# Gated mixing of two experts rewritten as (x + a) + g (e − a), with the experts' rows summed by TensorE

## The chip, the core and the metric

The kernel runs on one core of a Trainium2 chip. The metric is the device time of one execution in microseconds (us); the time before is the median of three runs, 3077.14 (3073.25 to 3079.84). A core has five engines with a queue of instructions each: TensorE (PE), VectorE (DVE), ScalarE (ACT), GpSimd (POOL) and SyncE (SP, which issues most transfers). They run side by side and wait for each other through semaphores. Within its own queue an engine takes instructions in order, so one that waits holds all that are queued behind it.

## The reference, cut to what matters

x has 2 batches of 2048 rows of 256. The first layer is attention plus a mixture of experts; the second is a selective state-space layer plus a ternary linear layer.

```python
xn = layernorm(x)
# first layer
x = x + attention(xn) + ffn(xn)
# ffn(x):
xn = layernorm(x) * ln_g + ln_b
abel = gelu(xn @ abel_w + abel_b)                      # "a" in the title
tw, ti = top_k(xn @ gate_w_moe + gate_b_moe, 2); tw = softmax(tw)
moe = sum over the two chosen experts of tw * expert(xn)
nonabel = moe @ rot                                    # "e" in the title
g = sigmoid(concat(abel, nonabel) @ mix_w + mix_b)
return x + abel * (1 - g) + nonabel * g
# second layer
xn = layernorm(x)
x = x + state_space(xn) + ternary_linear(xn)
```

The state-space layer projects xn to 1024 columns, convolves half of them over 4 rows, applies silu, derives a step size dt and vectors B and C, and runs h = exp(dt A) h + dt B x along the rows, for 16 states of each of 512 channels; y sums h C over the states.

## The kernel before, in words

The 4096 rows are 32 tiles of 128, handled as 8 chunks of 512 (QT = 4 tiles). There are four stages.

**First stage** (0 to 183 us). For each chunk it computes the normalised rows n1 and, normalised again, n2, transposes both, and makes q, k, v (q and k are stored to qk_d). The abel rows come from PE through a gelu on ACT (L308) into the tile ab. POOL multiplies ab by its part of mix_w (L311, tile am), DVE reduces that to one number a row (L314, sab), SP stores ab to ab_d (L315). POOL then adds n1 and the bias of the attention's projection to the x rows kept in SBUF (L316, L317). A scheduler makes the order on the engines here; the pools of the stage are given back at its end, and the first tiles of attention (L595 mask, L617 onesr) lie in that room.

**Attention and routing** (to about 1300 us) and the **experts** (to about 1920 us). The experts' results lie in y_d, one row for each token and chosen expert. The x rows with attention added are in xa_d.

**Mixing and state space** (L1148, 1920 to 3079 us). From L1784 on the order on every engine is the program's order. The work is 8 units of 512 rows (4 chunks by 2 batches), each of 16 steps, one per state. A step is: on ACT four decays exp(dt A) for the next step (L1729), on DVE a small add of the carried state (L1841), the scan over 128 x 2048 (L1843) and the product dt·x·B for the next step (L1753), on POOL a copy of the carry (L1854) and the product of the states with C (L1855), on PE the spreading of B's row for the product (L1740, tile bb) and the y sums (L1770).

Between these, three generators per unit are woven in by hand. `mix` makes the rows that enter the second layer, `ahead` the projections, convolution (L1446 on PE, L1455 on ACT, silu L1461), dt (L1535), B and C of the next unit, and `behind` the gate (L1590 on POOL) and the output of the unit before. The lists `kinds` and `kinds0` (L1657, L1672; the second for the first unit) name, for each generator, the step and quarter of a step at which it goes on to its next `yield`. A unit's mixing runs two units ahead of its scans, a gather of its rows (L1302, eight indirect transfers on POOL's queue) three ahead. The places of one unit's mixing:

| place (step, quarter) | what is issued in mix |
|---|---|
| (8,0) to (11,2), (14,1), (15,1), a unit earlier | gathers L1302, scaling by the router's weights on ACT L1311 |
| (0,2) | mo = sum of the two experts' rows on POOL, L1316; loads of ab and of the x rows xc |
| (3,2) and (4,0) | transposes of mo, L1327, first and second half |
| (4,2) | gate matmuls L1335, L1338, sigmoid on ACT L1348, L1349 |
| (7,1), (8,0) | reciprocal L1355, 1 − g on ACT L1356; pn = mo·rot L1362 in two halves, xc += g·pn on DVE L1369 |
| (8,0), (8,2) | ab scaled by 1 − g on ACT L1376; xc += ab on POOL L1379 |
| (9,1) to (12,3) | layer normalisation and transposes (L1384 to L1410) |

PSUM results of these flows take turns in two buffers (`mm`). What reads a result (a copy on ACT, say) is not issued with the matmuls but held by `issued` until the next result is issued, or until `settle`. So a result's reader stands in its engine's queue where the next one begins. The transposed rows moT take the place of the second expert's rows:

```python
moT = ys[:, 1].rearrange("p (k i) d -> p k (i d)", k=2)
```

The first two units' mixing runs ahead of the scans, the first one serially (1940 to 1957 us).

Of the kernel before, what the change touches and what calls it, by code (L numbers as in the profile page):

```python
# [13 lines left out]
AF = mybir.ActivationFunctionType  # L14
ALU = mybir.AluOpType
# [4 lines left out]
P = 128  # L20
# [13 lines left out]
TOP = 2  # L34
# [67 lines left out]
def tile_model(ctx: ExitStack, tc: tile.TileContext, t, out):  # L102
    nc = tc.nc
# [15 lines left out]
    ident = const.tile([P, P], F32, name="ident")  # L119
# [3 lines left out]
    rot = const.tile([P, 2, D], F32, name="rot")  # L123
# [27 lines left out]
    QT = CH // P  # L151
# [6 lines left out]
    with ExitStack() as c0:  # L158
# [5 lines left out]
        ab_d = scr.tile([P, NT, D], F32, name="ab_d")  # L164
# [3 lines left out]
        with tc.tile_pool(name="vs", bufs=1) as vsp, tc.tile_pool(name="qk", bufs=3) as qk:  # L168
# [6 lines left out]
            with tc.tile_pool(name="pa", bufs=2) as pa, tc.tile_pool(  # L175
# [4 lines left out]
                for c in range(NCH):  # L180
                    xg = xa[:, c * QT : (c + 1) * QT, :]
# [37 lines left out]
                for c in range(NCH):  # L219
                    xg = xa[:, c * QT : (c + 1) * QT, :]  # L220
# [13 lines left out]
                    for k in range(2):  # L234
                        p1 = pa_ps.tile([P, CH], F32, tag="tr", name=f"p1_{c}_{k}")
                        p2 = pa_ps.tile([P, CH], F32, tag="tr", name=f"p2_{c}_{k}")
                        for i in range(QT):
# [8 lines left out]
                            scale=col("ln_g")[:, k : k + 1],  # L246
                            bias=col("ln_b")[:, k : k + 1],
# [4 lines left out]
                    for i, name in enumerate(("q", "k")):  # L252
                        for m in range(2):
                            ps = pa_pa.tile([P, CH], F32, tag="ab", name=f"{name}_{c}_{m}")
                            for k in range(2):
                                nc.tensor.matmul(
                                    ps,
                                    lhsT=wd[i][:, k, m * P : (m + 1) * P],
                                    rhs=x1[:, k, :],
                                    start=(k == 0),  # L260
                                    stop=(k == 1),
                                )
                            parts = pa.tile([P, 2, CH], F32R, tag="parts", bufs=3, name=f"{name}p_{c}_{m}")
                            bias = bd[i][:, m : m + 1]
# [11 lines left out]
                    for h in range(2):  # L276
                        ps = pa_pa.tile([P, 2, D], F32, tag="ab", name=f"v_{c}_{h}")
                        for j in range(2):
                            at = (2 * h + j) * P
                            for k in range(2):  # L280
                                nc.tensor.matmul(
                                    ps[:, j, :],
                                    lhsT=x1[:, k, at : at + P],
                                    rhs=wv[:, k, :],
                                    start=(k == 0),
                                    stop=(k == 1),
# [9 lines left out]
                    ab = pa.tile([P, QT, D], F32, tag="ab", name=f"ab_{c}")  # L296
                    for i in range(QT):
                        ps = pa_pa.tile([P, D + E], F32, tag="ab", name=f"abp_{c}_{i}")
                        for k in range(2):
                            nc.tensor.matmul(  # L300
                                ps,
                                lhsT=x2[:, k, i * P : (i + 1) * P],
                                rhs=aw[:, k, :],
                                start=(k == 0),
                                stop=False,
# [4 lines left out]
                    am = pa.tile([P, QT, D], F32, tag="am", name=f"am_{c}")  # L310
# [1 line left out]
                        am, ab, row("mix_w")[:, 0:D].unsqueeze(1).to_broadcast([P, QT, D]), ALU.mult  # L312
                    )
                    nc.vector.tensor_reduce(sab[:, c * QT : (c + 1) * QT], am, AX.X, ALU.add)  # L314
                    nc.sync.dma_start(ab_d[:, c * QT : (c + 1) * QT, :], ab)  # L315
                    nc.gpsimd.tensor_tensor(xg, xg, n1, ALU.add)  # L316
                    nc.gpsimd.tensor_tensor(  # L317
                        xg, xg, row("b_proj").unsqueeze(1).to_broadcast([P, QT, D]), ALU.add
                    )
# [828 lines left out]
def mix_and_state_space(tc, t, col, row, ident, ones, rot, routes, sab, rw, y_d, ab_d, xa_d, out_tiles):  # L1148
# [10 lines left out]
    nc = tc.nc  # L1159
    NC = S // CH  # L1160
    QT = CH // P
# [5 lines left out]
    with ExitStack() as ctx:  # L1167
# [80 lines left out]
        ps = ps_m.tile([P, 1], F32, tag="mm", name="absum")  # L1248
# [20 lines left out]
        def settle(n=0):  # L1269
            while len(held) > n:  # L1270
                take, ps = held.pop(0)
                take(ps)
# [21 lines left out]
        def mix(at):  # L1294
# [14 lines left out]
            for e in range(TOP):  # L1309
# [2 lines left out]
                        ys[:, e, i, :], ys[:, e, i, :], AF.Copy, scale=wts[:, e, n0 + i : n0 + i + 1]  # L1312
                    )
                yield
            mo = ys[:, 0]
            nc.gpsimd.tensor_tensor(mo, mo, ys[:, 1], ALU.add)  # L1316
            ab = one.tile([P, QT, D], F32, tag="k", name=f"ab_{u}")
            nc.sync.dma_start(ab, ab_d[:, n0 : n0 + QT, :])
            xc = m_["xc"] = xcp.tile([P, QT, D], F32, tag="xc", name=f"xc_{u}")
# [4 lines left out]
            for k in range(2):  # L1324
                ps = mm(f"moT_{u}_{k}")
                for i in range(QT):
                    nc.tensor.transpose(  # L1327
                        ps[:, i * P : (i + 1) * P], mo[:, i, k * P : (k + 1) * P], ident
                    )
                issued(ps, lambda ps, k=k: nc.scalar.copy(moT[:, k, :], ps))  # L1330
                yield
            settle()

            ps = mm(f"gate_{u}", (P, QT))
            nc.tensor.matmul(ps, lhsT=ident, rhs=sab[:, n0 : n0 + QT], start=True, stop=False)  # L1335
            for i in range(QT):
                for k in range(2):
# [4 lines left out]
                        start=False,  # L1342
# [10 lines left out]
            settle()  # L1353
            yield
            nc.vector.reciprocal(g[:, 0, :], g[:, 1, :])  # L1355
            nc.scalar.activation(g[:, 1, :], g[:, 0, :], AF.Identity, scale=-1.0, bias=1.0)  # L1356
            for h in range(2):
                ps = mm(f"pn_{u}_{h}", (P, 2, D))
                for i in range(2):
                    ts = slice((2 * h + i) * P, (2 * h + i + 1) * P)  # L1360
                    for k in range(2):
                        nc.tensor.matmul(  # L1362
                            ps[:, i, :], lhsT=moT[:, k, ts], rhs=rot[:, k, :], start=(k == 0), stop=(k == 1)
                        )

                def add(ps, h=h):
                    for i in range(2):
                        n = 2 * h + i
                        nc.vector.scalar_tensor_tensor(  # L1369
                            xc[:, n, :], ps[:, i, :], g[:, 0, n : n + 1], xc[:, n, :], ALU.mult, ALU.add  # L1370
                        )

                issued(ps, add)
                yield
            for i in range(QT):
                nc.scalar.activation(ab[:, i, :], ab[:, i, :], AF.Copy, scale=g[:, 1, i : i + 1])  # L1376
            yield
            settle()
            nc.gpsimd.tensor_tensor(xc, xc, ab, ALU.add)  # L1379
            yield  # L1380

            mv = one.tile([P, QT, 2], F32, tag="mv", bufs=2, name=f"mv3_{u}")
# [584 lines left out]
```

## Time and profile before

| what | us | share of the span |
|---|---|---|
| median of the runs | 3077.14 | |
| the profiled execution | 3080.93 | |
| its span | 3079.2 | |
| PE busy | 2634.9 | 86% |
| DVE busy | 2043.7 | 66% |
| ACT busy | 1592.4 | 52% |
| POOL busy | 1187.6 | 39% |

By stages, busy time of the engines and the granted clock of PE (1 is full speed):

| stretch, us | PE | DVE | ACT | POOL | clock |
|---|---|---|---|---|---|
| 0 to 183 | 144.0 | 106.5 | 73.3 | 60.0 | 0.95 |
| 183 to 1300 | 1015.8 | 860.2 | 653.9 | 175.6 | 0.95 |
| 1300 to 1920 | 601.7 | 104.7 | 162.0 | 98.9 | 0.99 |
| 1920 to 2014 | 50.5 | 29.6 | 39.1 | 24.0 | 0.69 |
| 2014 to 3057 | 806.0 | 942.7 | 662.3 | 824.2 | 0.80 |

A row of groups reads: line, engine, operation, tile written <- tiles read, shapes, count | busy us, mean ns | idle time before it and what ended most of it. A row of waits reads: engine, tile and line that waited <- engine, tile and line waited for: us in total, times, longest. A row of a timeline reads: start us, duration us, engine, line, operation, count and, in brackets, idle time before it and what ended that. A row of stretches has, for each of PE, PE's weight loads, DVE, ACT and POOL, the busy us and the number of instructions, then the granted clock, DMA's share and GB/s.

### The profile page before, as it was taken

To read this page: it belongs to the slowest core of one execution; us is meant where nothing else is said; L and a number is where in the kernel's file an instruction comes from. 1 tells how busy PE (TensorE), PEld (TensorE's weight loads), DVE (VectorE), ACT (ScalarE), POOL (GpSimd) and SP (SyncE) were. 2 spreads that over 40 slices of the span, in tenths; PEclk is the share of its full clock that TensorE was granted. 3 is DMA by queue.
4 is the path that set the end of the run, shared out by engine and by line. 5 is a ranking of instruction groups with operands and counts; after the bars stand their busy time and mean duration, and the time that the engine had idled before them with its cause. 6 is when DMAs were issued, how large, how long until landed. Compare 5 with 4: busy or idle time off the path is not lost. (4 is left out here: it accounts for less than half of the span.)

```text
span 3079.2 us, 39986 instructions
## 1 busy us (share of the span) xinstructions
PE 2634.9 (86%) x15021; PEld 1493.3 (48%) x15021; DVE 2043.7 (66%) x2558; ACT 1592.4 (52%) x2546; POOL 1187.6 (39%) x934
## 2 busy tenths in 40 slices
PE   6887888999999999799999999577778888788747
PEld 4543433445444444488888888333333343333303
DVE  6576766888788888324111011258999999999996
ACT  3424555666566666422222222456766676666643
POOL 4313223010111011111111111247887978878775
PEclk9978988999999999899999999677887888879758
DMA  8843214112232220434345553323544535445350
GB/s 290 214 133 80 57 51 86 29 29 42 50 48 29 29 29 1 151 134 144 133 150 194 183 193 109 77 54 85 120 111 104 131 78 133 110 102 117 82 116 14
DMA packets 120614, 309.58 MB, mean 101 GB/s; under 512 B 28464, under 2 KB 70832, under 8 KB 102880
## 3 DMA queue, kind: packets, MB, share of 16 engines
q1 hardware_dynamic: 100496, 206.57, 28.3%
q0 software_dynamic: 18576, 99.24, 9.6%
q8 instruction: 122, 2.00, 0.3%
q10 hardware_dynamic: 1344, 1.16, 0.1%
q14 instruction: 76, 0.62, 0.1%
HBM read 228.51 MB, written 78.38 MB: 100 GB/s over the span
## 5 line engine op out<-in xcount | busy, mean ns | idle before, releaser
L758 ACT ACTIVATE p<-s 128x1024 f32<-128x1024 f32 (+3 forms) x640 | 563.2, 900 | 382.4 <-PE s L750 361.5
L665 DVE TENSOR_REDUCE best<-m 128x2 f32<-128x1024 f32 (+3 forms) x640 | 669.6, 1062 | 111.6 <-PE m L652 101.0
L1855 POOL TENSOR_TENSOR hh<-hh,cc 128x2048 f32<-128x2048 f32 x128 | 579.9, 4531 | 10.3
L1843 DVE TENSOR_TENSOR_SCAN hh<-decay,uh 128x2048 f32<-128x2048 f32 x128 | 565.9, 4421 | 23.8 <-ACT decay L1729 10.1
L705 PE MATMUL pv<-p,v 128*17 128x256 f32 (+1 forms) x4608 | 383.8, 379 | 49.0 <-POOL p L763 46.1
L763 POOL TENSOR_SCALAR_AFFINE_SELECT p<-p 128x256 f32<-128x256 f32 x256 | 103.3, 408 | 785.6 <-ACT p L758 784.5
L1729 ACT ACTIVATE decay<-dd,a_neg 128x511 f32<-128x511 f32 x512 | 332.9, 712 | 53.4 <-DVE hh L1843 52.8
L1118 ACT ACTIVATE hT<-h,b1s 128x256 f32<-128x256 f32 x296 | 137.7, 473 | 384.3 <-PE h L1111 384.3
L1132 DVE TENSOR_TENSOR yt<-o,b 128x512 f32<-128x512 f32 x37 | 25.6, 692 | 436.9 <-PE o L1124 436.9
L1753 DVE TENSOR_TENSOR uh<-dd,bb 128x2048 f32<-128x2048 f32 x128 | 293.6, 2294 | 21.5 <-PE bb L1740 11.6
L750 PE MATMUL s<-q,k 64*128 64x512 f32 (+3 forms) x1280 | 288.2, 437 | 22.9 <-DVE best L665 17.6
L652 PE MATMUL m<-k,q 64*128 64x512 f32 (+3 forms) x1280 | 281.6, 426 | 17.6 <-DVE best L665 8.9
L1111 PE MATMUL h<-xT,w 128*128 128x256 f32 x1184 | 276.1, 387 | 19.7 <-ACT hT L1118 8.1
L1124 PE MATMUL o<-w,hT 128*128 128x256 f32 x1184 | 262.7, 380 | 0.0
L1074 POOL DMA_INDIRECT w<-in_w,wrow x74 | 71.1, 961 | 479.2 <-PE h L1111 255.5
L1111 PEld LDWEIGHTS h<-xT,w 128*128 128x128 f32 x1184 | 226.7, 193 | 54.8 <-ACT hT L1118 8.5
L750 PE MATMUL s<-tops,onesr 64*128 64x512 f32 (+3 forms) x1280 | 248.5, 371 | 0.0
L1124 PEld LDWEIGHTS o<-w,hT 128*128 128x128 f32 x1184 | 225.7, 191 | 30.9
L1770 PE MATMUL y<-hh,sel 128*32 128x512 f32 x1024 | 162.1, 710 | 78.8 <-POOL hh L1855 78.6
L705 PEld LDWEIGHTS pv<-p,v 128*17 128x17 f32 x4608 | 107.9, 97 | 232.4 <-issue 113.5
L750 PEld LDWEIGHTS s<-q,k 64*128 64x128 f32 x1280 | 127.0, 188 | 168.1 <-DVE best L665 56.6
L652 PEld LDWEIGHTS m<-k,q 64*128 64x128 f32 x1280 | 129.3, 192 | 131.7 <-ACT p L758 68.1
(341 smaller groups left out, 3477.2 us busy)
## 6 DMA issues: line engine op xcount, KB each, us to landing
dd<-dd_d SPq DMA_DIRECT2D x120, 512.0 KB, 7.1
q<-qk_d SPq DMA_DIRECT2D x128, 128.0 KB, 5.1
k<-qk_d SPq DMA_DIRECT2D x128, 128.0 KB, 7.5
x_d<-zero SPq DMA_DIRECT2D x6, 1664.0 KB
xg<-x_d SPq DMA_DIRECT2D x37, 256.0 KB, 6.6
y_d<-yt SPq DMA_DIRECT2D x37, 256.0 KB
qk_d<-qp SPq DMA_DIRECT2D x16, 512.0 KB, 7.3
qk_d<-kp SPq DMA_DIRECT2D x16, 512.0 KB, 4.0
```

The costliest lines, as they stand in the source:

```text
L652: nc.tensor.matmul(ps[:, h, 0:n], lhsT=qT[hs, qs], rhs=kT[hs, c * CH : c * CH + n], start=True, stop=True, tile_position=(HP * h, 0),)
L665: nc.vector.tensor_reduce(best[:, i, :, c], ps[:, :, 0:n], AX.X, ALU.max)
L705: nc.tensor.matmul(pv[r0 : r0 + HS + 1, lo - f * HC : HC], lhsT=v[:, b * TPB + kb, 2 * pr + h, :], rhs=pt[:, h, lo:hi], start=(kb == 0), s ...
L750: nc.tensor.matmul(ps[:, h, off:CH], lhsT=(kT[hs, kb * P : (kb + 1) * P], onesr[hs, :])[i], rhs=(qT[hs, j * CH + off : (j + 1) * CH], tp[h ...
L758: nc.scalar.activation(pt[:, :, off:CH], ps[:, :, off:CH], AF.Exp, scale=float(HS) ** -0.5)
L1111: nc.tensor.matmul(ph, lhsT=w1[:, k * DF + f * P : k * DF + (f + 1) * P], rhs=xT[:, k, :], start=(k == 0), stop=(k == 1),)
L1124: nc.tensor.matmul(po[:, h, :], lhsT=hT[:, f, h * P : (h + 1) * P], rhs=w2[:, f * D : (f + 1) * D], start=(f == 0), stop=(f == NF - 1),)
L1729: nc.scalar.activation(decay[G % 2][:, q, 1:], of[at]["dd", n // 4][:, 0, q, 1:], AF.Exp, scale=a_neg[:, q, n : n + 1],)
L1753: nc.vector.tensor_tensor(uh, of[at]["dd", n // 4][:, 1], of[at]["bb", n].to_broadcast(full), ALU.mult)
L1770: nc.tensor.matmul(of[at]["y"][C4 * q : C4 * (q + 1), :], lhsT=sel, rhs=hh[:, q, :], start=False, stop=(g == 3), tile_position=(0, C4 * q),)
L1843: nc.vector.tensor_tensor_scan(hh.rearrange("p q c -> p (q c)"), decay[G % 2].rearrange("p q c -> p (q c)"), uh.rearrange("p q c -> p (q c)"),
L1855: nc.gpsimd.tensor_tensor(hh, hh, m_["cc", g].to_broadcast(full), ALU.mult)
```

## The change

The mixed row is x + a + g (e − a) in place of x + g e + (1 − g) a. The first stage adds a to the x rows that it keeps (POOL) and stores −a in place of a (negated on ACT, into the tile am). In the mixing, pn becomes the sum of −a, by a matmul with the identity, and of the product with rot, both in PSUM; 1 − g, the four scalings of ab and the addition of ab to xc go. The addition of the two experts on POOL goes too: each transpose of their sum becomes two matmuls with the identity, which add up in PSUM. Both halves are now issued at the place (3,2), and the place (4,0) has nothing of the mixing.

```diff
@@ first stage
                     nc.vector.tensor_reduce(sab[:, c * QT : (c + 1) * QT], am, AX.X, ALU.add)
-                    nc.sync.dma_start(ab_d[:, c * QT : (c + 1) * QT, :], ab)
+                    nc.scalar.activation(am, ab, AF.Copy, scale=-1.0)
+                    nc.sync.dma_start(ab_d[:, c * QT : (c + 1) * QT, :], am)
                     nc.gpsimd.tensor_tensor(xg, xg, n1, ALU.add)
+                    nc.gpsimd.tensor_tensor(xg, xg, ab, ALU.add)
@@ mix
-            mo = ys[:, 0]
-            nc.gpsimd.tensor_tensor(mo, mo, ys[:, 1], ALU.add)
...
             for k in range(2):
                 ps = mm(f"moT_{u}_{k}")
                 for i in range(QT):
-                    nc.tensor.transpose(
-                        ps[:, i * P : (i + 1) * P], mo[:, i, k * P : (k + 1) * P], ident
-                    )
+                    for e in range(TOP):
+                        nc.tensor.matmul(
+                            ps[:, i * P : (i + 1) * P],
+                            lhsT=ys[:, e, i, k * P : (k + 1) * P],
+                            rhs=ident,
+                            start=(e == 0),
+                            stop=(e == TOP - 1),
+                        )
                 issued(ps, lambda ps, k=k: nc.scalar.copy(moT[:, k, :], ps))
-                yield
+            yield
+            yield
             settle()
...
             nc.vector.reciprocal(g[:, 0, :], g[:, 1, :])
-            nc.scalar.activation(g[:, 1, :], g[:, 0, :], AF.Identity, scale=-1.0, bias=1.0)
...
                     ts = slice((2 * h + i) * P, (2 * h + i + 1) * P)
+                    nc.tensor.matmul(
+                        ps[:, i, :], lhsT=ident, rhs=ab[:, 2 * h + i, :], start=True, stop=False
+                    )
                     for k in range(2):
                         nc.tensor.matmul(
-                            ps[:, i, :], lhsT=moT[:, k, ts], rhs=rot[:, k, :], start=(k == 0), stop=(k == 1)
+                            ps[:, i, :], lhsT=moT[:, k, ts], rhs=rot[:, k, :], start=False, stop=(k == 1)
                         )
...
-            for i in range(QT):
-                nc.scalar.activation(ab[:, i, :], ab[:, i, :], AF.Copy, scale=g[:, 1, i : i + 1])
             yield
             settle()
-            nc.gpsimd.tensor_tensor(xc, xc, ab, ALU.add)
             yield
```

## The prediction

> **What bounds the kernel now.** I read the page's busy shares and slices, then its costliest groups, the waits of VectorE (DVE), a table by stretches, and timelines. The state-space stage is the last third, from the first scan at 2014 to 3057 us. The change touches that stage, its prologue (1940 to 2014) and the first stage (0 to 187); attention and experts between them are only displaced. Costliest groups that matter, from the page:
>
> ```profile
> L1855 POOL TENSOR_TENSOR hh<-hh,cc 128x2048 f32<-128x2048 f32 x128 | 579.9, 4531 | 10.3
> L1843 DVE TENSOR_TENSOR_SCAN hh<-decay,uh 128x2048 f32<-128x2048 f32 x128 | 565.9, 4421 | 23.8 <-ACT decay L1729 10.1
> ...
> L1753 DVE TENSOR_TENSOR uh<-dd,bb 128x2048 f32<-128x2048 f32 x128 | 293.6, 2294 | 21.5 <-PE bb L1740 11.6
> ```
>
> 128 steps of 4.42 (scan) + 2.29 (product) + 0.17 (add) + some 0.25 of hand-over make 7.1 us: DVE sets the pace. The stretches view, 2300 to 2500 us, agrees:
>
> ```profile
> 2300.00:2500.00 200.00, 167.06 (x534) 70.25 (x534) 184.54 (x99) 134.80 (x208) 161.92 (x87) 0.82 0.48 115
> ```
>
> DVE is busy 184.5 of 200, POOL 161.9, TensorE (PE) 167.1. Work taken from POOL or ACT therefore pays only where DVE waits for it. Those waits, 2170 to 2950 us:
>
> ```profile
> DVE uh L1753 <- PE bb L1740: 11.1, 11, 1.5
> DVE hh L1843 <- ACT decay L1729: 9.9, 6, 3.0
> DVE xc L1369 <- PE pn L1362: 3.1, 4, 1.4
> ```
>
> About 25 us in all, hardly one named POOL; POOL stands behind PE's part where PE's y sums (L1770) wait for hh (45.8 us in 2100 to 2900) and bb queues behind them. The groups of PE in that stretch show the mixing, and on what it waits:
>
> ```profile
> L1362 PE MATMUL pn<-rot,ys 128*128 128x256 f32 x96 | 35.7, 536 | 0.0
> ...
> L1338 PE MATMUL gate<-rw,ys 128*128 128x1 f32 x96 | 21.3, 343 | 16.4 <-ACT ys L1330 16.4
> ...
> L1327 PE MATMUL moT<-ident,ys 128*128 128x128 f32 x48 | 8.8, 311 | 0.0
> ```
>
> In these 6 units pn's 8 matmuls a unit left 96 records and the 8 transposes 48: an fp32 matmul leaves two records, an fp32 transpose one.
>
> **The transposing sums on PE.** 8 transposes a unit become 16 matmuls, and both halves are issued at place (3,2). At full clock, records of 128 columns start 110 ns apart (4 transposes: 3×0.11+0.33 = 0.66 us in units 1 to 5). Thirty-two take 31×0.11+0.33 = 3.74 us where 0.66 stood before the first copy. In cold records (210 ns) it is 6.9. What this meets, in unit 3, on ACT and then DVE:
>
> ```profile
> 2467.22 0.58 ACT L1330 COPY ys<-moT 128x512 f32<-128x512 f32 x1 [0.89 <-PE moT L1327]
> 2467.83 1.28 ACT L1461 ACT_TABLE_LOAD   x1
> 2469.12 1.91 ACT L1461 ACTIVATE xs<-xs 128x2048 f32<-128x2048 f32 x1
> 2471.04 1.28 ACT L1729 ACT_TABLE_LOAD   x1
> 2472.33 2.56 ACT L1729 ACTIVATE decay<-dd,a_neg 128x511 f32<-128x511 f32 x4
> 2474.80 0.56 ACT L1330 COPY ys<-moT 128x512 f32<-128x512 f32 x1
> ```
> ```profile
> 2475.79 0.17 DVE L1841 TENSOR_TENSOR uh<-uh,c 128x4 f32<-128x4 f32 x1
> 2476.07 4.42 DVE L1843 TENSOR_TENSOR_SCAN hh<-decay,uh 128x2048 f32<-128x2048 f32 x1
> ```
>
> The decays of step 5 end at 2474.89, the scan that needs them starts at 2476.07: 1.18 us of slack. In the changed order ACT's queue has both copies ahead of the silu. The second waits for the burst's end, and the first is held too: it writes half of ys[:,1], which the burst still reads. Queued behind are table, silu, table, four decays. They come 3.74−0.66 = 3.1 us later. Slack is 1.15 to 1.18 in units 1, 3, 4 and none in 2 and 5 (decay end 2347.63, scan 2347.66). Loss: 3×1.95 + 2×3.1 = +12 us at full clock; with records of 210 ns 3×5.1+2×6.2 = +28. I take +12, since all transposes in these units ran at 0.66. POOL's mo add goes ahead of the burst, and with it ACT's copies of cv (14.5 us of waits for POOL's zs) come up to 2.36 earlier; but the last cv stands on PE behind a bb that waits for DVE (2461.47 in unit 3), so the burst doesn't start earlier.
>
> The Trainium skill ("TensorE: Matmul & The Clock Gate", Terms) speaks against this edit: transpose mode is four times faster for FP32. By it one matmul costs four transposes, the burst 64×0.11 = 7.0 us, and the loss 3×5.2+2×6.4 = +28 (an estimate from that page and the 110 ns). The row shows two records per fp32 matmul against one, each of 256 columns starting 220 ns after the last as each transpose of 128 does after 110; the trace decides, a factor of 2. No run here has an fp32 matmul of 128 columns, so +28 stays inside the range.
>
> What comes back: the gate matmuls no longer wait for a second copy that is queued behind the decays. That wait is the 16.4 us of the row above, 2.7 to 4.4 a unit. Starting earlier, the xp, dt, bb, pn chain on PE gains as much, and DVE's gaps at steps 6 and 7 (1.9, 1.6, 0.3, 1.9, 1.6 us in units 1 to 5, 7.2 in all) mostly close: −6.3. The four added matmuls of pn per half (8 records, 0.22 each hot, 0.43 cold) are 1.8 to 3.4 a unit of this lead; PE has some 33 idle us in 200, and I charge nothing unless the lead fails (below).
>
> **What POOL and ACT lose.** Per unit POOL drops two adds of 2.36, ACT a small g and four scalings of 0.49. POOL's products trail the scan by 3.3 to 3.9 us at steps 9 and 10 and by 8.5 at 11; the xc add is one cause. PE's y sum waits for it and the following bb comes 1.2 to 1.4 late at step 13. I take 0.9 back in four units: −3.6 (ends: 0, where the gathers hold POOL, and −6). In unit 0 the one wait of DVE's bn_stats for POOL's xc (1.8 at 2154.7) goes partly: −1.5. Another such wait (5.8 near the first steps) gives nothing: a chain over dt ends at 2050.3 anyway.
>
> **The prologue** is serial: moT at 1942.0 (1.95 us), gate 1943.8 to 1947.8, pn 1947.7 to 1953.2, DVE's xc, POOL's xc 1954.26 for 2.34, bn_stats 1956.6. The burst starts cold, some 5.45 (between 3.74 and 6.9): +3.7 at the gate's end after the pipelined copies; pn gains 8 records, +1.6; POOL's add goes, −2.5. Sum +2.8 (0 to +5). The second chunk's burst lies ahead of other waiting and is hidden.
>
> **The first stage.** Eight times POOL gets one add (2.35), ACT one negation (1.02 by the 128x1024 row of L758), and SP's store of it starts later. In mid-stage the negation waits for DVE's reduce and holds ACT about a microsecond, the store comes some 4.7 later, and the loads of q and k queue behind it on SP; PE or the other stores are later still, so hidden. One row bears on the added POOL adds: a DVE scaling of 128x256 (L144) has a median of 0.406 and a worst of 1.765, ending as a POOL add ended. "Advanced Engine Details and Errata" of the skill (GPSIMD Details) says why: POOL shares a read and a write interface with DVE. Its rule would stall DVE over each of eight adds, up to 8×1.4 = 11; the trace has one or two such outliers in some 24 POOL adds. I take +1.5 (0 to +5).
>
> The end is exposed. POOL's queue, then DVE's:
>
> ```profile
> 179.56 2.34 POOL L311 TENSOR_TENSOR am<-ab,rows 128x1024 f32<-128x1024 f32 x1 [12.01 <-ACT ab L308]
> 183.26 0.29 POOL L595 MEMSET mask<- 128x128 f32 x1 [1.36 <-DMA q<-qk_d]
> ```
> ```profile
> 181.93 1.22 DVE L314 TENSOR_REDUCE sab<-am 128x4 f32<-128x1024 f32 x1 [2.25 <-POOL am L311]
> 183.19 0.23 DVE L617 CAST onesr<-ones 128x128 fp32r<-128x128 f32 x1
> ```
>
> Attention's first tiles lie where the first stage's pools were, and start when the last user is done: the reduce, at 183.15. Now POOL still has +ab to 184.3 and the bias to 186.6, and ACT's negation ends at 184.2 with its store landing by 187.9. The mask waits for ACT and DMA, onesr for POOL and ACT. +3.5 to +4.7, taken +4, and DVE runs without gaps behind it, so it carries to the end.
>
> **Sum.** 1.5 + 4 + 2.8 − 1.5 + 12 − 6.3 − 3.6 = +8.9. The profiled run took 3080.93 (span 3079.2 and 1.7 around it), so 3089.8 on its footing; that run lies 3.8 above the median of 3077.14, from which I forecast 3086.
>
> **Rivals,** each with its chance.
> - *Slow burst* (0.18): fp32 matmuls of 128 columns take 0.21 a record or four passes. The term 12 becomes 28: 3102. For it: cold stretches, granted clock 0.82 in the table. Against: 0.66 in every steady unit.
> - *PE lead fails* (0.12): the longer burst and pn eat the gate's lead, DVE waits for pn and bb at steps 6 to 7 stay. Without the −6.3 and with 0.9 more in each of four units: 3085.9 + 6.3 + 3.6, about 3096.
> - *Faster by a freed POOL* (0.20): it decides on POOL's lag behind the scan at step 11. Falls that from 8.5 below 4, by all that is dropped, then hh is in time for every y sum: the bb and pn waits (11.1 + 3.1) and the small ones (1.5) close, and in unit 0 both POOL waits (5.8 + 1.8). With the burst's 12, the prologue's 2.8, and the hand-over absorbed later by attention: −15.7 − 7.6 + 14.8 = −8.5, 3069. Against: the gathers hold POOL in the same steps, and the waits name PE and ACT.
> - *Nothing measurable* (0.20): the stall at step 5 lets POOL and PE catch up, so that it costs 12 and returns as much from later steps (the 14.2 of bb and pn instead of my 9.9); prologue and first stage at their low ends, 0 and +3.5: 12 − 14.2 + 3.5 − 1.5 = 0, 3077.
> - *Likeliest as summed* (0.30): 3082 to 3092.
>
> The measurement tells 0.2% (6.2 us) from no change, so faster means below 3071, slower above 3083.3. Faster 0.20, same 0.20, slower 0.60 (0.30 + 0.18 + 0.12). The range goes from the freed POOL's to the slow burst's time, 3068 to 3103, and leaves out the far half of each.
>
> **What would show it.** In the changed trace: the moT burst at step 3 near 3.7 us with 32 records (6.9 or 7 is the slow rival); the scan of step 5 waiting for decay 2 to 3 us in each of units 1 to 5; the gate free of ACT's copy and steps 6 and 7 without gaps; onesr near 187; POOL's lag at step 11 under 8. I am wrong if scan 5 starts on time, if POOL's lag falls by its whole 4.7, or if DVE's tensor_scalars in the first stage lengthen under POOL's adds.

## The result, and the profile after

The changed kernel takes 3094.04 us (median of 5 runs, 3091.30 to 3100.57), the kernel before in the same comparison 3076.23 (5 runs, 3073.06 to 3079.84). The ratio is 1.0064, 95% interval 1.0048 to 1.0080: slower by about 18 us. Forecast were 3086, a loss of 9, and a range up to 3103. The direction and the range held; the loss is twice the forecast and lies above the 3082 to 3092 that was given as likeliest.

The profiled execution took 3093.74 (span 3092.0). Code lines lie 5 or 6 lower here than before: the scan L1843 is now L1849, the product L1759, the decays L1735, the copies of moT L1335. The groups of the page:

```profile
L1849 DVE TENSOR_TENSOR_SCAN hh<-decay,uh 128x2048 f32<-128x2048 f32 x128 | 565.9, 4421 | 37.6 <-ACT decay L1735 24.0
L1861 POOL TENSOR_TENSOR hh<-hh,cc 128x2048 f32<-128x2048 f32 x128 | 580.0, 4531 | 11.0 <-PE y L1776 0.4
...
L1759 DVE TENSOR_TENSOR uh<-dd,bb 128x2048 f32<-128x2048 f32 x128 | 293.7, 2295 | 16.4 <-PE bb L1746 7.0
```

Durations are those of before to the nanosecond or two. What moved is idle time: the scan's wait for the decays went from 10.1 to 24.0, the product's wait for PE's bb from 11.6 to 7.0. The waits of DVE between 2170 and 2970 us say the same of the steady units:

```profile
DVE hh L1849 <- ACT decay L1735: 23.8, 10, 3.8
DVE uh L1759 <- PE bb L1746: 4.9, 7, 1.8
DVE xc L1378 <- PE pn L1371: 3.1, 2, 2.3
```

PE's groups of the mixing, 2100 to 2900 us:

```profile
L1371 PE MATMUL pn<-rot,ys 128*128 128x256 f32 x96 | 34.1, 493 | 0.0
L1328 PE MATMUL moT<-ident,ys 128*128 128x128 f32 x192 | 25.5, 296 | 0.0
L1367 PE MATMUL pn<-ab,ident 128*128 128x256 f32 x48 | 21.9, 550 | 0.0
L1345 PE MATMUL gate<-rw,ys 128*128 128x1 f32 x96 | 11.7, 250 | 0.9 <-ACT ys L1335 0.9
```

192 records for 96 matmuls in six units: two for each fp32 matmul. The gate's wait for the copy is gone, 16.4 to 0.9.

A timeline of ACT in unit 3, and DVE's scan behind it:

```profile
2477.09 0.58 ACT L1335 COPY ys<-moT 128x512 f32<-128x512 f32 x1 [3.18 <-PE moT L1328]
2477.98 0.59 ACT L1335 COPY ys<-moT 128x512 f32<-128x512 f32 x1 [0.31 <-PE moT L1328]
2478.58 1.28 ACT L1467 ACT_TABLE_LOAD   x1
2479.88 1.91 ACT L1467 ACTIVATE xs<-xs 128x2048 f32<-128x2048 f32 x1
2481.81 1.28 ACT L1735 ACT_TABLE_LOAD   x1
2483.10 2.56 ACT L1735 ACTIVATE decay<-dd,a_neg 128x511 f32<-128x511 f32 x4
```
```profile
2485.69 4.42 DVE L1849 TENSOR_TENSOR_SCAN hh<-decay,uh 128x2048 f32<-128x2048 f32 x1 [2.15 <-ACT decay L1735]
```

Both copies stand ahead of the silu, the first of them idle for 3.18 us while the burst runs, and the scan of step 5 comes 2.15 late. In unit 2 it is 3.85. The difference is one of PE's clock, as two timelines of PE show:

```profile
2337.74 5.40 PE L1452 MATMUL cv<-xr,taps 128*128 128x512 f32 x8
2343.07 1.06 PE L1776 MATMUL y<-hh,sel 128*32 128x512 f32 x8
2344.07 3.84 PE L1328 MATMUL moT<-ident,ys 128*128 128x128 f32 x32
...
2469.48 3.70 PE L1452 MATMUL cv<-xr,taps 128*128 128x512 f32 x8
2473.11 1.07 PE L1776 MATMUL y<-hh,sel 128*32 128x512 f32 x8
2474.10 3.84 PE L1328 MATMUL moT<-ident,ys 128*128 128x128 f32 x32
```

The burst takes 3.84 in both. The convolution block ahead of it took 5.40 in unit 2, with a granted clock of 0.68, and 3.70 in unit 3, with 1.00.

The stretch from 2300 to 2500 us has DVE busy 180.05 where it was 184.54, and less work on ACT and POOL:

```profile
2300.00:2500.00 200.00, 166.71 (x584) 71.34 (x583) 180.05 (x92) 129.95 (x202) 153.38 (x82) 0.87 0.47 111
```

The end of the first stage, in timelines of POOL and of DVE:

```profile
187.61 2.35 POOL L318 TENSOR_TENSOR xa<-xa,ab 128x1024 f32<-128x1024 f32 x1
190.04 2.34 POOL L319 TENSOR_TENSOR xa<-xa,rows 128x1024 f32<-128x1024 f32 x1
193.53 0.20 POOL L597 MEMSET mask<- 128x128 f32 x1 [1.15 <-DMA ab_d<-am]
```
```profile
187.68 1.22 DVE L314 TENSOR_REDUCE sab<-am 128x4 f32<-128x1024 f32 x1 [2.26 <-POOL am L311]
193.51 0.44 DVE L619 CAST onesr<-ones 128x128 fp32r<-128x128 f32 x1 [4.61 <-DMA ab_d<-am]
```

The reduce is 5.75 later than before, and onesr, which followed it at once, now waits 4.61 more, last for the store of −a.

Where the profiled execution's 12.8 us went, by landmarks in the two traces:

| stretch | before | after | difference |
|---|---|---|---|
| first stage, to the end of its last reduce L314 | 183.15 | 188.90 | +5.75 |
| from there to attention's onesr | 0.04 | 4.61 | +4.57 |
| attention, to the end of its last pv matmul | 1091.3 | 1090.0 | −1.3 |
| to the end of the experts' last matmul | 645.4 | 641.9 | −3.5 |
| to the first scan | 94.3 | 94.5 | +0.1 |
| first scan to end of the last | 1038.3 | 1043.0 | +4.8 |
| behind the last scan | 26.7 | 29.1 | +2.4 |

The experts' row is not the change's. From the first to the last matmul of the experts it was 630.1 before and 624.3 after, and between 626.0 and 630.0 in nine of the runs below that leave that stage alone. This execution was quick there by some 5 us. Nor is the 12.8 the loss: the profiled execution of before lies 4.7 above its median, this one at its own. Rows of single executions carry several us of chance. The stretch from the first scan to the last took 1038.3 and 1032.2 in two executions with the mixing of before (the second is that of the last experiment), and 1038.8 to 1044.7 in the five that have the instructions of the changed mixing: about +6.5 on the mean, where the table has +4.8.

### The profile page after: what moved, and what is told of

The parts are those of the page before. It is cut to its first block, busy times and chain, and to the rows that moved or that the text cites. A ratio compares the mean times of both kernels' runs of the same rounds, so it can differ in the third digit from the quotient of the medians.

```text
span 3092.0 us, 40438 instructions
## 1 busy us (share of the span) xinstructions
PE 2654.0 (86%) x15277; PEld 1517.0 (49%) x15277; DVE 2050.8 (66%) x2558; ACT 1586.3 (51%) x2514; POOL 1170.8 (38%) x926
## 5 line engine op out<-in xcount | busy, mean ns | idle before, releaser
L1849 DVE TENSOR_TENSOR_SCAN hh<-decay,uh 128x2048 f32<-128x2048 f32 x128 | 565.9, 4421 | 37.6 <-ACT decay L1735 24.0
L1735 ACT ACTIVATE decay<-dd,a_neg 128x511 f32<-128x511 f32 x512 | 332.1, 711 | 61.9 <-DVE hh L1849 61.1
L1759 DVE TENSOR_TENSOR uh<-dd,bb 128x2048 f32<-128x2048 f32 x128 | 293.7, 2295 | 16.4 <-PE bb L1746 7.0
```

The source lines that it names most:

```text
L1735: nc.scalar.activation(decay[G % 2][:, q, 1:], of[at]["dd", n // 4][:, 0, q, 1:], AF.Exp, scale=a_neg[:, q, n : n + 1],)
L1759: nc.vector.tensor_tensor(uh, of[at]["dd", n // 4][:, 1], of[at]["bb", n].to_broadcast(full), ALU.mult)
L1849: nc.vector.tensor_tensor_scan(hh.rearrange("p q c -> p (q c)"), decay[G % 2].rearrange("p q c -> p (q c)"), uh.rearrange("p q c -> p (q c)"),
```

## The experiments

Each was timed beside the kernel before; its ratio stands with its interval. "Index n" is the gap of DVE between the end of scan n and the next scan, less what it works in it; its floor is 0.2 to 0.3. Sums of gaps are over units 1 to 5.

**The first stage taken back.**

```diff
-                    nc.scalar.activation(am, ab, AF.Copy, scale=-1.0)
-                    nc.sync.dma_start(ab_d[:, c * QT : (c + 1) * QT, :], am)
+                    nc.sync.dma_start(ab_d[:, c * QT : (c + 1) * QT, :], ab)
-                    nc.gpsimd.tensor_tensor(xg, xg, ab, ALU.add)
```

> The changed kernel with the first stage as it was before: a is stored unnegated and not added to the x rows, so the mixed row here is x + g (e + a), not the reference's. Theory (the first stage costs about 10 us: POOL's added adds keep DVE's scalings L144 from starting, +5.7, and POOL's last adds hold the pools that attention's first tiles wait for, +4.5): onesr starts near 183.2 again, attention's end comes about 9 us earlier than in the changed kernel, L144's mean falls from 834 to about 450 ns, the time is about 3084. Rival (the loss lies in the mixing alone, TensorE's burst and its clock; the first stage's shift is absorbed later): 3092 to 3094.

3083.71, ratio 1.0027 (1.0012 to 1.0041). The last reduce ends at 181.8, onesr follows at once, attention ends 10.5 us before that of the changed kernel, and the median is 10.3 lower. So the first stage is about 10 of the 18 us. In four executions with the first stage of before the reduce ends at 181.3 to 183.2, in six that have the changed one's addition on POOL at 187.2 to 189.5. L144, a scaling of 128x256 on DVE, in the changed kernel (first) and in this one (second), with minimum, median and maximum in ns:

```profile
L144 DVE TENSOR_SCALAR n<-xa,mv_a,ra x32: 400/410/2511, 13.1 to 126.4; 128x256 f32<-128x256 f32 x32
```
```profile
L144 DVE TENSOR_SCALAR n<-xa,mv_a,ra x32: 400/407/1785, 12.5 to 117.5; 128x256 f32<-128x256 f32 x32
```

The median hides it; the means are 834 and 450 ns. In one chunk of the changed kernel, POOL and DVE:

```profile
82.23 2.36 POOL L311 TENSOR_TENSOR am<-ab,rows 128x1024 f32<-128x1024 f32 x1 [7.89 <-ACT ab L308]
84.55 2.37 POOL L318 TENSOR_TENSOR xa<-xa,ab 128x1024 f32<-128x1024 f32 x1
87.00 2.35 POOL L319 TENSOR_TENSOR xa<-xa,rows 128x1024 f32<-128x1024 f32 x1
```
```profile
85.76 4.39 DVE L144 TENSOR_SCALAR n<-xa,mv_a,ra 128x256 f32<-128x256 f32 x4
```

Four scalings of 0.4 each take 4.39 us and are done at 90.1, just after the last addition ends at 89.35. In the traces of before and after, no L144 lay inside a POOL addition. The last four chunks of the changed kernel all meet this. Their pace, taken at the end of the four scalings from the fourth chunk to the eighth, is 19.4 us a chunk; it was 17.1 before and is 17.1 in this run. That is 9.1 us over the four chunks; 1.3 less ahead of them and 2.1 less behind leave the 5.75.

**The negation taken out**, by turning the sign of rot and of g instead.

```diff
-                    nc.scalar.activation(am, ab, AF.Copy, scale=-1.0)
-                    nc.sync.dma_start(ab_d[:, c * QT : (c + 1) * QT, :], am)
+                    nc.sync.dma_start(ab_d[:, c * QT : (c + 1) * QT, :], ab)
...
+        nc.vector.tensor_scalar(rot, rot, -1.0, None, ALU.mult)
...
-                nc.scalar.activation(g[:, 1, :], g[:, 0, :], AF.Identity, bias=1.0)
+                nc.scalar.activation(g[:, 1, :], g[:, 0, :], AF.Identity, scale=-1.0, bias=minus)
```

> The changed kernel without the negation on ACT: a is stored as it is, and rot and g change sign instead (one DVE operation ahead of the state-space stage). POOL's add of a stays. Theory (POOL's adds are the cost): L144 stays near 830 ns, the first stage's last reduce stays near 188.9, onesr starts when POOL's last add is done, about 1 us earlier than 193.5; the time is about 3093. Rival (the negation on ACT and the late store of -a are the cost): the last reduce goes back to 183 and onesr to some 186, the time is 3084 to 3086.

3096.61, ratio 1.0061 (1.0044 to 1.0077): no gain. The last reduce still ends at 188.0 and L144's mean is 823, so it is the addition and not the negation that slows the stage. onesr starts at 189.03, 1.1 after the reduce, and I had that wrong by 3.5: it waits for POOL's addition of a and no longer for its addition of the bias. But a small operation of DVE just behind it (L865, 0.25 us before) then took 2.45 us, until that last addition was done, and attention's first reduce came 2.2 earlier than in the changed kernel. So onesr is 4.5 earlier and the time is no lower: that the hand-over's 4.57 reach the end is not shown by this run.

**VectorE adds a in the first stage.**

```diff
-                    nc.gpsimd.tensor_tensor(xg, xg, ab, ALU.add)
+                    nc.vector.tensor_tensor(xg, xg, ab, ALU.add)
```

> The changed kernel with the first stage's eight additions of a done by VectorE instead of GpSimd; the negation stays. Theory (POOL's adds, back to back, keep DVE's scalings from starting): L144's mean falls from 834 to under 500 ns though DVE has 8 additions more, the last reduce ends by 185 instead of 188.9, onesr starts by 189 instead of 193.5, the time is 3086 to 3089. Rival (it is the added work and its place in the chunk, whoever does it): the last reduce stays at 188 or later, 3093 to 3098.

3089.56, ratio 1.0046 (1.0030 to 1.0061). L144's mean falls to 520, the reduce ends at 183.0, onesr starts at 187.44. At first sight as forecast. But the pace from the fourth chunk to the eighth is only down to 18.8, 2.3 of the 9.1 us, and the stage catches up behind them. There SP's queue differs by one transfer: of the six that fill x_d with zeros (1664 KB each), the sixth was issued at 126 to 135 us in the twelve other kernels, ahead of loads of q and k; here the scheduler put it beside the fifth, at 80.1. SP's queue in this run and in the next one:

```profile
79.47 3.04 SPq L229 DMA_DIRECT2D x_d<-zero  x2
```
```profile
131.24 0.69 SPq L229 DMA_DIRECT2D x_d<-zero  x1
```

Behind it ACT's writing of k waits for the stores of q, again in this run and in the next one:

```profile
152.65 0.69 ACT L265 ACTIVATE kp<-k,bkd 128x512 fp32r<-128x512 f32 x1 [1.46 <-DMA qk_d<-qp]
```
```profile
156.50 0.69 ACT L265 ACTIVATE kp<-k,bkd 128x512 fp32r<-128x512 f32 x1 [9.02 <-DMA qk_d<-qp]
```

The twelve kernels with the late transfer all wait 6.6 to 9.1 us there, and take 61.6 to 64.4 us from the eighth chunk's scalings to the last reduce; this one takes 58.5. No run moves that transfer alone, but the early end at 183.0 can't be put down to VectorE's additions. DVE's own additions are longer where a POOL operation runs, and onesr still waits for the store:

```profile
178.51 3.39 DVE L318 TENSOR_TENSOR xa<-xa,ab 128x1024 f32<-128x1024 f32 x1
181.83 1.21 DVE L314 TENSOR_REDUCE sab<-am 128x4 f32<-128x1024 f32 x1
187.44 0.30 DVE L619 CAST onesr<-ones 128x128 fp32r<-128x128 f32 x1 [4.41 <-DMA ab_d<-am]
```

POOL's am ran from 178.48 to 180.83 meanwhile.

**Both: VectorE adds, no negation** (rot and g change sign as above).

```diff
-                    nc.scalar.activation(am, ab, AF.Copy, scale=-1.0)
-                    nc.sync.dma_start(ab_d[:, c * QT : (c + 1) * QT, :], am)
+                    nc.sync.dma_start(ab_d[:, c * QT : (c + 1) * QT, :], ab)
-                    nc.gpsimd.tensor_tensor(xg, xg, ab, ALU.add)
+                    nc.vector.tensor_tensor(xg, xg, ab, ALU.add)
...
```

> The changed kernel with VectorE's additions of a in the first stage and without the negation (rot and g change sign): both causes taken from the first stage at once. Theory (hand-over: what attention's first tiles wait for are POOL's last additions, and behind them the store of the negated rows): the last reduce ends near 183 as with VectorE's additions alone, and onesr, which started 4.4 us after it there, starts within 2.5 of it, near 185; the time is 3 less than with VectorE's additions alone, about 3086. Rival (the pools are held by something else, such as the loads of q and k): onesr stays at 187 and the time at 3089 to 3090.

3093.21, ratio 1.0053 (1.0038 to 1.0068). The hand-over went as expected and beyond: onesr starts 0.04 after the reduce. The time did not: the reduce itself ends at 188.1, with the pace (18.9) and L144 (525) as in the run before, but the sixth transfer of zeros in its late place. Here POOL is the one that waits:

```profile
183.49 3.39 POOL L311 TENSOR_TENSOR am<-ab,rows 128x1024 f32<-128x1024 f32 x1 [8.65 <-ACT ab L308]
```

DVE's addition began at 183.47. These operations with two operands in SBUF ran one after the other on the two engines, whichever began first. So the addition costs the chunks their pace on either engine: on DVE it hardly lengthens L144 (520 and 525 ns against 450) or POOL's run of additions, but takes its own time from both. The 5 us between the ends of these two runs lie behind the chunks' scalings (58.5 and 64.2 us to the last reduce), where that transfer stands. What holds onesr is shown: the store of −a held it for 4.4 us, and without the negation and POOL's addition nothing does. What that is worth is not: onesr is 5.3 earlier than in the changed kernel, and the time, 3093.21 against 3094.04, is the same within the intervals.

**The burst earlier.**

```diff
-            [(0, 2), (3, 2), (4, 0), (4, 2), (5, 2), (7, 1), (8, 0), (8, 0), (8, 2), (9, 1), (10, 2)]
+            [(0, 2), (1, 2), (4, 0), (4, 2), (5, 2), (7, 1), (8, 0), (8, 0), (8, 2), (9, 1), (10, 2)]
```

> The changed kernel with the burst of 32 transposing matmuls issued at (1,2) instead of (3,2); nothing else moves. Theory (the burst costs what it holds up on ACT: both copies stand ahead of the silu and of step 5's decays): the waits of the scan for decays at index 4 of units 1 to 5, 15.7 us in sum, fall to about 2, no other wait grows by more than 3 in sum, and the time falls by 8 to 13 to about 3084. Rival (TensorE itself is short of time or of clock with 256 more records): the wait only moves to another step, 3091 to 3095.

3092.47, ratio 1.0048 (1.0031 to 1.0065). My theory failed here. The gaps at index 4 did fall from 15.7 us to 1, but the gaps at index 7 rose from 4.7 to 12.6 and one at index 2 to 2.7. The waits of DVE, 2170 to 2960 us:

```profile
DVE hh L1849 <- ACT decay L1735: 11.0, 5, 3.1
DVE xc L1378 <- PE pn L1371: 10.2, 4, 3.1
DVE uh L1759 <- PE bb L1746: 7.1, 12, 2.5
```

The wait moved from ACT's decays to PE's pn; the 11.0 for decays that are left lie at index 15. The table by stretches, from the end of scan 4 to the start of scan 8 in unit 2, tells why: kernel before, changed kernel, this one.

```profile
2344.10:2371.70 27.60, 23.55 (x67) 11.00 (x67) 24.79 (x15) 19.34 (x31) 18.32 (x10) 0.63 0.29 65
```
```profile
2348.90:2380.50 31.60, 27.39 (x79) 11.54 (x75) 24.79 (x15) 23.58 (x33) 19.24 (x10) 0.68 0.30 65
```
```profile
2354.60:2382.40 27.80, 26.56 (x79) 12.58 (x75) 24.74 (x15) 16.68 (x26) 19.27 (x10) 0.66 0.33 74
```

In the last, PE is busy 26.56 of 27.80 us (96%) at a granted clock of 0.66. Over units 1 to 5 these stretches sum to 135.9 before, 147.4 after and 141.0 here. Take away the stall on ACT and PE is the bound of those four steps.

**The burst in two halves by rows**, each copied into that part of the second expert's rows that only it reads.

```diff
-            for k in range(2):
-                ps = mm(f"moT_{u}_{k}")
-                for i in range(QT):
-                    for e in range(TOP):
+            for h in range(2):
+                ps = mm(f"moT_{u}_{h}")
+                for k in range(2):
+                    for i in range(2):
+                        for e in range(TOP):
...
-            yield
-            yield
+                yield
```

> The changed kernel with the burst cut by rows into two of 16 matmuls, one at (3,2), one at (4,0), each copied into the part of the second expert's rows that only it reads. By the first theory (copies ahead of the silu): the waits for decays at index 4 fall from 15.7 us in sum to 3 to 6. By the second (TensorE's work from step 3 to step 7 is what is late): the waits at index 7 grow by nearly as much, to 10 or more, as with the early burst, and the time falls by no more than 3, to 3091 to 3094. If only the first holds, it falls by 8 to 12.

3088.16, ratio 1.0037 (1.0025 to 1.0050), between the two forecasts. Index 4 falls to 8.2 (0.5 to 1.3 in units with a quick convolution block, 2.2 and 3.7 in the others), index 7 rises to 11.6. Both causes are at work.

**Without −a in pn.**

```diff
-                    nc.tensor.matmul(
-                        ps[:, i, :], lhsT=ident, rhs=ab[:, 2 * h + i, :], start=True, stop=False
-                    )
...
```

> The changed kernel without pn's four matmuls of -a by the identity (the mixed row is then x + a + g e, not the reference's). Theory, as the earlier burst left it (the wait went from step 5's decays to pn at index 7, so between the burst and pn it is TensorE's own work that is late): with 16 records less a unit the waits of DVE for pn in units 2 and 4, 2.2 us each, fall under 1, and the time falls by 3 to 5 to 3089 to 3091. Rival (pn's added matmuls are hidden, only the place of the burst matters): no wait changes by more than 0.5, 3093 to 3095.

3089.90, ratio 1.0046 (1.0029 to 1.0063), 4 less, as expected; its interval overlaps that of the changed kernel, so the gaps carry the argument. (The records taken out are 8 a unit, 48 in six units by the row above, and not the 16 that I wrote.) The gaps at index 7 are 0.7 at most, in all units, though in this execution the convolution block was slow in each of them and index 4 was at 3.9 to 4.0.

**The experts' sum back on GpSimd.**

```diff
+            mo = ys[:, 0]
+            nc.gpsimd.tensor_tensor(mo, mo, ys[:, 1], ALU.add)
...
-                    for e in range(TOP):
-                        nc.tensor.matmul(
...
+                    nc.tensor.transpose(
+                        ps[:, i * P : (i + 1) * P], mo[:, i, k * P : (k + 1) * P], ident
+                    )
```

> The changed kernel with the experts' sum back on POOL (L1316 of before) and transposes of it, a half at (3,2) and one at (4,0); the first stage and -a in PSUM stay. Theory: scans of index 4 wait 2 us in sum instead of 15.7, the gate waits for the second copy behind the decays again (16 us) and what had come back at steps 6, 7 and 13 goes by about half: the time falls by 5 to 8, to 3086 to 3089. Rival (the sum on TensorE pays, the added matmuls of pn are what costs): no fall, or a rise, 3094 to 3098.

3086.23, ratio 1.0030 (1.0018 to 1.0043): 7.8 less, at the good end. Index 4 sums to 2.2, first scan to last is 1033.5. That is 9.5 below the changed kernel; against the kernel before it is no gain, since that mixing took 1038.3 in one execution and 1032.2 in another.

**The sum by TensorE alone**, in the kernel before.

```diff
-            mo = ys[:, 0]
-            nc.gpsimd.tensor_tensor(mo, mo, ys[:, 1], ALU.add)
...
-                    nc.tensor.transpose(
...
+                    for e in range(TOP):
+                        nc.tensor.matmul(
...
```

> The kernel before with one part of the change alone: the experts' sum by TensorE in one burst at (3,2), no sum on GpSimd; first stage, the ab scalings and the xc addition as before. Theory (the parts add up: the change less the sum put back was 7.8 us of the 17.8, the first stage 10.3, the rest of the mixing about nothing): 3082 to 3086. The scans at index 4 wait 2.3 us in a unit whose last convolution block ran at full clock (3.70 us) and 4.0 where it took 5.40; the gap at index 13 stays at 1.4 to 1.9, since it hangs on the xc addition that GpSimd keeps. Rival (the sum costs only together with pn's added matmuls, TensorE being short between steps 3 and 7): 3076 to 3079, with what is lost at index 4 made up at 6 and 7.

3086.35, ratio 1.0027 (1.0016 to 1.0037). Alone it costs 8 to 10 us, as much as taking it away from the whole gave back. Its index 4 is 2.3 behind a block of 3.70 us (unit 4; 3.1 in unit 1) and 3.9 to 4.0 behind one of 5.1 to 5.4; index 13 stays at 1.3 to 1.8. The waits of DVE, 2170 to 2960 us:

```profile
DVE hh L1847 <- ACT decay L1733: 26.7, 11, 3.8
DVE uh L1757 <- PE bb L1744: 7.0, 7, 1.4
DVE xc L1373 <- PE pn L1366: 0.5, 1, 0.5
```

The waits at index 6 and 7 come to 0.5 us in sum; they were 7.2 in the profile of before and 3.8 in another execution of its mixing (the last experiment). With the burst but without pn's added matmuls, what I expected back at these steps does come back. It does not pay for the 15 us more at index 4.

**What seemed to pay, put together:** the first stage of before, a added to the x rows on DVE in the experts' stage, −a in PSUM by the turned signs, the sum on GpSimd.

```diff
@@ experts, against the kernel before
+            nc.sync.dma_start(at, ab_d[:, cs, :])
+            nc.vector.tensor_tensor(xa[:, cs, :], xa[:, cs, :], at, ALU.add)
             nc.sync.dma_start(xa_d[:, cs, :], xa[:, cs, :])
...
```

The stores to xa_d, which stood ahead of the experts, go in between their tiles with the additions.

> The parts that paid, put together: the first stage as before (a stored as it is, no addition), a added to the x rows on VectorE during the experts' stage, -a in PSUM by a negated rot and g, the experts' sum back on GpSimd with transposes in two halves. Theory: first stage and onesr as before (183), from the first scan to the last 1033 to 1035 us as with the sum put back (before 1038.3), the additions hidden behind the experts, prologue shorter by 2: 3069 to 3074, ahead of before by 3 to 8. Rival (what seemed gained in the scans was chance of the clock, or the additions hold up the experts): 3076 to 3082.

3076.87 against 3075.90, ratio 1.0004 (0.9997 to 1.0011, 20 runs). A miss: the algebra shows no gain even when its first-stage price is not paid, though it frees an addition of 2.36 on POOL and four scalings on ACT in each unit. Index 13 gains 0.6 to 1.1 a unit (3.3 in all), and index 7, ahead of which PE has eight more records, goes from 5.0 in sum to 9.8. From the first scan to the last it took 1033.4, as forecast; but the next run, with the mixing of before, took 1032.2, so this was no sign of a gain.

**One GpSimd addition less in the kernel before:** the bias of the projection added on DVE in the experts' stage.

```diff
-                    nc.gpsimd.tensor_tensor(
-                        xg, xg, row("b_proj").unsqueeze(1).to_broadcast([P, QT, D]), ALU.add
-                    )
...
+            nc.vector.tensor_tensor(
+                xa[:, cs, :], xa[:, cs, :], row("b_proj").unsqueeze(1).to_broadcast([P, CH // P, D]), ALU.add
+            )
             nc.sync.dma_start(xa_d[:, cs, :], xa[:, cs, :])
...
```

> The kernel before, with one GpSimd addition less per chunk in the first stage: the projection's bias is added on VectorE in the experts' stage. It asks whether the cost found in the first stage also runs the other way. Theory (POOL's adds keep DVE's small operations from starting; five of some 1.3 us instead of 0.15 and two scalings of 1.77 in the kernel before): the long tensor_scalars of DVE fall from 6 to 2 or 3, the last reduce ends 1 to 3 us before 183.2, the time is 3073 to 3076. Rival (they are hidden behind TensorE and the transfers there): the reduce ends at 183, 3076 to 3078.

3073.95 against 3076.19, ratio 0.9992 (0.9982 to 1.0002): not told from no change (the stores to xa_d move as in the run before). DVE's scalings of over a microsecond in the first stage fall from five to two. The last reduce ends at 182.2, 1.0 before 183.2, but three other runs with the first stage of before end it at 181.3 to 181.8, so nothing is gained there: the cost does not run the other way.

## Why the prediction was half the loss

Point by point, with the terms of the sum:

- *The burst* (32 records, 3.74 us at full clock): 3.84 in every steady unit. Two records per fp32 matmul held; four transposes to a matmul, 7.0 us, an estimate that I had made from the Trainium skill ("TensorE: Matmul & The Clock Gate", Terms), did not, and with them the slow rival fell.
- *Loss at step 5* (+12): the gaps at index 4 grew by 13.5. Place, cause and size held. Which units have no slack was not fixed: it follows the granted clock in the convolution block ahead, 2.3 after 3.70 us (3.1 in unit 1) and 4.0 after 5.40, and differs from execution to execution.
- *What comes back at steps 6 and 7* (−6.3): −1.9 in the profile. This is the first step that failed, by a term that I put at nothing. I said that PE had "some 33 idle us in 200" and charged pn's added matmuls nothing. Between scans 4 and 8, where they lie, PE was busy 85 to 94% in the kernel before, at a granted clock of 0.63 to 0.69. The earlier burst, the halves and the run without −a in pn showed PE as the bound there. The burst without these matmuls gave 6.7 back at these steps (3.3 against the other execution of that mixing); the matmuls without the burst ("What seemed to pay") lengthened index 7 by 4.8. So the way back was right, and these matmuls took most of it, four to five us. (The prediction says "four per half"; they are four a unit, and its 8 records are right for a unit.)
- *The rival "PE lead fails"*, 3096: it named this step. That 3094 lies near it is chance: it also gives up the −3.6 of POOL's lag, which did come, and has nothing of the first stage's excess.
- *POOL's lag* (−3.6): index 13 gave 3.3, and the lag at step 11 went from 8.5 to 7.7. The cause held too: index 13 sums to 2.7 to 3.5 in every run without the xc addition, and to 6.1 to 6.7 in the three that keep it. The rival of a freed POOL fell: it needed less than 4.
- *Unit 0* (−1.5): the gap with the wait for POOL's xc, at index 12, went from 2.6 to 0.8, and stays at 2.6 in the two runs that keep the xc addition. *Prologue* (+2.8): 0 in this profile; from PE's absum to the first scan, profiles with the same prologue range from 70 to 76 us, so nothing can be said of a term this small.
- *First stage* (+1.5, range 0 to 5): +5.75, outside its own bounds. This is the second step that failed, with as large an error as the first. That DVE's scalings lengthen under POOL's adds was one of my signs of being wrong, and they did. I had the row (a scaling of 1.765, which lay across POOL's multiplication L311) and the rule of the Trainium skill's "Advanced Engine Details and Errata" (GPSIMD Details), from which I had put the cost at up to 11, and counted outliers instead of asking where the new addition would stand: back to back with two others, at the time of the next chunk's scalings, so that DVE finds no gap. The rule was the better guide: DVE's scalings took 32 × (834 − 450) ns = 12.3 us longer, and 5.75 reached the end of the stage.
- *Hand-over* (+4): 4.57. The run with neither negation nor POOL's addition has none. That it reaches the end is shown only together with the 5.75, by the first stage taken back. The two runs without the negation have onesr 4.5 and 5.3 earlier and are no faster; attention, 1088.5 to 1097.9 us in the thirteen profiles, varies too much to follow 4 us through it.

With these values the sum of the prediction comes to about 17.

By single parts, from the ratios: first stage 11 us (1.0064 against 1.0027), sum by TensorE 8 (1.0027 alone), the algebra in the mixing 1 (1.0004; the additions in the experts' stage are in it). They add up to 20 against 20 measured by that ratio (0.0064 × 3076). Each carries an interval of 2 to 7 us to either side, so that they agree this closely is luck.

Open is what the first stage's cost would be in another order: the scheduler places its transfers anew for each edit, and two runs that differ only in the negation ended it 5 us apart, with one transfer in another place.

## What to carry to other kernels

Read an engine's slack in the steps where the new work will stand, at the clock granted there, and not over a stage: 83% busy on the mean was 85 to 94% in four steps of sixteen before anything was added. Before giving GpSimd one more addition, look at what VectorE does at that moment; several in a row shut it out. A reader of PSUM queued ahead of a table load and a decay makes everything behind it wait for the whole burst, and moving the burst only shows the next bound. Where a scheduler makes the order, compare the order of the transfers before a difference of a few us is put down to the edit, and keep two profiles of the same code: here its stretches differed by as much as what was to be explained.

## What the runs showed of the hardware

A 128x1024 addition on VectorE took 1.22 us undisturbed and 3.39 when GpSimd had begun a multiplication of that size 0.03 us before; GpSimd's multiplication took 2.35 undisturbed and 3.39 when VectorE's addition had begun 0.02 us before. A 128x256 fp32 scaling on VectorE (0.406 us) never lay inside a GpSimd addition or multiplication of that size, while 29 of its BATCH_NORM_STATS2 and 28 of its BATCH_NORM_AGGREGATE did in the changed kernel. One transfer of 1664 KB of zeros ahead of the loads of q and k went with a wait of ScalarE for a store of q of 6.6 to 9.1 us in twelve kernels; in the one where it stood elsewhere, that wait was 1.5.
